# Layer 2 of a fused graph network: the reciprocal root by Sqrt and reciprocal instead of Ln, Exp and a Newton step

## The chip, the cores and the metric

The kernel runs on one core of one Trainium2 chip. The core has a matrix engine (TensorE, PE in the profile), VectorE (DVE), ScalarE (ACT), GpSimd (POOL) and a queue for transfers (SyncE, SP). The metric is the device time of one launch in microseconds (us), lower is better. The kernel before takes 2618.51 us, the median of 3 runs (2617.28 to 2624.15).

## The reference

The input is a batch of 32 graphs with 512 nodes of 64 features each, an adjacency matrix of 512 x 512 per graph (symmetric in its pattern), and a node mask. Four graph layers follow one another for each graph, with residuals and layer norms between them:

- layer 0 multiplies by the degree-normalised adjacency,
- layer 1 is a Chebyshev filter of order 4,
- layer 2 is hyperbolic attention: for every pair of nodes a logarithmic map, its attention weight, and a weighted sum,
- layer 3 takes weighted quantiles of each node's neighbours.

The change lies in layer 2 alone. What it must compute for a pair is

```
sub = mobius_add(-p1, p2, c)
sub_norm = maximum(norm(sub), 1e-15)
log = 2 / lambda(p1) * arctanh(clip(sub_norm, -1 + 1e-7, 1 - 1e-7)) * sub / sub_norm
```

So a norm, its reciprocal, and an inverse hyperbolic tangent are needed for each of the 512 x 512 pairs. The kernel gets all of them from two products per pair: with E a squared distance and X = E times a denominator, the norm is E/sqrt(X), and the inverse tangent is half the difference of two logarithms, ln(1 + s) - ln(1 - s). The function is symmetric in the two nodes, so only the upper block triangle is worked out: 1280 columns for the 128 rows of a tile, in two parts of 640.

## The kernel before

The 32 graphs are independent until the end. For each graph the program records some 1,100 operations in several lanes: `front` (layers 0 and 1), `pairs` and `tail` (layer 2), `graph` (the adjacency pattern, ranks and slots that layer 3 needs), `gather` and `sort` (bringing the neighbours' values together and sorting them in a network of minima and maxima), and, for each two graphs, `head` (quantiles and the last dense layers). Nothing is issued while recording. The class `Order` then lays out all operations of all graphs in one list per engine: `issue` (line 295) steps through a model of five clocks, gives each operation a cost that its helper states (line 445 for VectorE, 482 for ScalarE, 504 for TensorE, 468 for GpSimd), and takes, on the engine whose clock is earliest, the ready operation with the earliest due time. Due times come from `STAGES` (line 1415) and a period of 80 us for each graph. The order found is pinned, so on the chip each engine works through its list strictly in order, and waits at an instruction whose inputs are not there. Where the model sees TensorE idle, it writes filler products in (lines 1451 to 1454). The helpers' lines (448, 452, 455, 461 on VectorE, 471, 475 and 722 on GpSimd, 483 on ScalarE, 502 and 507 on TensorE) are the lines of the profile, so operations are told apart by their tiles.

The stated costs take part in the program only through the order. `recip` (line 460) costs what any f32 operation of one element per cycle costs, 0.07 us + 1.04 ns per element.

ScalarE works with one set of function tables at a time. The field `table` of an operation names the set that it needs; where the model sees a change it adds 1.28 us, and `issue` writes a load of the set with both exponential and logarithm ahead of a switch to "exp" (line 391). Loads of the set for Sigmoid and Tanh are put in by the compiler.

In `pairs` (lines 969 to 1092), per graph:

- lines 1005 to 1014: two logarithms on a 128 x 4 tile (`lp`, `sn`), then four GpSimd operations that end in `oo`, the bias of the Sigmoid on line 1077.
- lines 1038 to 1046: TensorE gives the distances; ScalarE writes E, VectorE writes X, over four blocks of rows.
- lines 1049 to 1052: in both parts of 640 columns, ScalarE writes R = exp(-0.5 ln(X + tiny)) and W = 0.5 R squared.
- lines 1053 to 1060: VectorE makes one Newton step, R = (W X - 1.5) R, whose sign comes out negative; then E = E R, and the clip as a maximum with -1 + 1e-7. ScalarE takes the two logarithms from it.
- lines 1061 to 1092: the difference of the logarithms times R gives Q; then logits, Sigmoid, adjacency, and the weighted sum.

The tiles EX, RW, FT, Q of this lane have one buffer each.

Of the kernel before, what the change touches and what calls it, by code (L numbers as in the profile page):

```python
# [8 lines left out]
F32 = mybir.dt.float32  # L9
# [5 lines left out]
AF = mybir.ActivationFunctionType  # L15
OP = mybir.AluOpType
# [4 lines left out]
P = 128  # L21
# [159 lines left out]
class Order:  # L181
# [41 lines left out]
            self.masks[key] = m  # L223
        return a.tensor.name, p, p + a.ap[0][1], m

    def op(self, engine, issue, tail, fn, outs, ins, table=None):

        if not self.on:
            fn()
            return  # L230
        i = len(self.ops)
        deps, names = {}, set()
        for a, write in [(a, False) for a in ins] + [(a, True) for a in outs]:
            if a is None or not isinstance(a, bass.AP) or a.space == DRAM:
                continue
            name, p0, p1, m = self.region(a)
            if name in self.tiles:
                names.add(name)
            elif name not in self.seen and not write:
                continue  # L240
            w, r = self.seen.setdefault(name, ([], []))
            for e in w:
                if e[2] & m and e[0] < p1 and p0 < e[1]:
                    deps[e[3]] = True
            if write:
                for e in r:
                    if e[2] & m and e[0] < p1 and p0 < e[1]:
                        deps.setdefault(e[3], False)
                for k in (w, r):
                    for e in k:  # L250
                        if p0 <= e[0] and e[1] <= p1:
                            e[2] &= ~m
                    k[:] = [e for e in k if e[2]]
                w.append([p0, p1, m, i])
            else:
                r.append([p0, p1, m, i])
        if engine == "PE":

            name, p0, p1, _ = self.region(outs[0])
            g = self.groups.setdefault(name, [])  # L260
            for e in g:
                if e[0] < p1 and p0 < e[1]:
                    deps.setdefault(e[2], False)
            g[:] = [e for e in g if not (p0 <= e[0] and e[1] <= p1)] + [(p0, p1, i)]
        deps.pop(i, None)
        for n in names:
            self.tiles[n][2] += 1
        self.ops.append((engine, issue, tail, fn, deps, names, (self.lane, self.batch), table))

    def due(self, period, stage):  # L270


        end, depth, longest = [0.0] * len(self.ops), [0.0] * len(self.ops), {}
        for i, (e, issue, tail, _, deps, _, where, _) in enumerate(self.ops):
            t = 0.0
            for d, full in deps.items():
                if self.ops[d][6] == where:
                    t = max(t, self.after(d, i, end[d], full))
            depth[i] = t
            end[i] = t + issue  # L280
            longest[where] = max(longest.get(where, 0.0), t + issue)
        key = []
        for i, o in enumerate(self.ops):
            (lane, b), (lo, hi) = o[6], stage[o[6][0]]
            key.append(period * (b + lo + (hi - lo) * depth[i] / longest[o[6]]))
        return key
# [8 lines left out]
    def issue(self, period, stage, filler, fill):  # L295
        import heapq

        ops, n = self.ops, len(self.ops)
# [16 lines left out]
        table = None  # L315
# [4 lines left out]
        while len(order) < n:  # L320
            best = None
            for e in self.ENGINES:
                t = clock[e] if ready[e] or e == "PE" and any(shapes.values()) else max(clock[e], coming[e][0][0]) if coming[e] else None
# [3 lines left out]
            t, e = best  # L327
            clock[e] = t
            while coming[e] and coming[e][0][0] <= t:
                i = heapq.heappop(coming[e])[1]  # L330
                heapq.heappush(shapes.setdefault(ops[i][7], []) if e == "PE" else ready[e], (key[i], i))
            if e == "PE":
                pick = min((h[0][0] + (0.0 if c == shape else self.STAY), c) for c, h in shapes.items() if h)[1]
                i = heapq.heappop(shapes[pick])[1]
            else:
                i = heapq.heappop(ready[e])[1]
            engine, issue, tail, fn, deps, names, where, tab = ops[i]
# [24 lines left out]
            elif tab is not None and tab != table:  # L362
                switch, table = True, tab
# [18 lines left out]
        before, spare = {}, 0.0  # L382
        for t, _, i, tab in sorted(order):
            e, fn = ops[i][0], ops[i][3]
            if e == "PE":

                for _ in range(int((t - spare - fill) / 0.11)):
                    before[e] = self.pin(filler(), before.get(e))
                spare = t + ops[i][1]
            if tab == "exp":  # L390
                before[e] = self.pin(self.nc.scalar.preload_act_table_set("natural_log_exp_and_others"), before.get(e))
            before[e] = self.pin(fn(), before.get(e))
        self.span = max(clock.values()), order

# [9 lines left out]
def tile_adj_resnorm(ctx: ExitStack, tc: tile.TileContext, x, adj, nodemask, w1k, b1k, att_w, att_b,  # L404
                     w1, b1, w2, b2, out):
    nc = tc.nc
# [12 lines left out]
    const = ctx.enter_context(tc.tile_pool(name="const", bufs=1))  # L419
# [5 lines left out]
    seq = Order(nc, tc)  # L425
# [21 lines left out]
    def tt(out, a, b, op):  # L447
        vec(lambda: nc.vector.tensor_tensor(out, a, b, op=op), out, [a, b])  # L448

    def ts(out, a, s1, s2, op0, op1=None):  # L450
        kw = {} if op1 is None else {"op1": op1}
        vec(lambda: nc.vector.tensor_scalar(out, a, s1, s2, op0=op0, **kw), out, [a], True, (s1, s2))  # L452

    def stt(out, a, s, b, op0, op1):
        vec(lambda: nc.vector.scalar_tensor_tensor(out, a, s, b, op0=op0, op1=op1), out, [a, b], False, (s,))  # L455
# [4 lines left out]
    def recip(out, a):  # L460
        vec(lambda: nc.vector.reciprocal(out, a), out, [a])
# [4 lines left out]
    def gp(f, out, ins):  # L466

        seq.op("POOL", 1.0, 0.5, f, [out], ins)

    def gtt(out, a, b, op):  # L470
        gp(lambda: nc.gpsimd.tensor_tensor(out, a, b, op=op), out, [a, b])

    def gts(out, a, s1, s2, op0, op1=None):
        kw = {} if op1 is None else {"op1": op1}
        gp(lambda: nc.gpsimd.tensor_scalar(out, a, s1, s2, op0=op0, **kw), out, [a] + [x for x in (s1, s2) if isinstance(x, bass.AP)])

    def act(out, a, f, bias=None, scale=1.0, accum_out=None, after=None):
        sc = [x for x in (bias, scale) if isinstance(x, bass.AP)]
        kw = {k: v for k, v in (("bias", bias), ("accum_out", accum_out)) if v is not None}
        n = width(out)  # L480
        table = "exp" if f in (AF.Ln, AF.Exp) else "sig" if f in (AF.Sigmoid, AF.Tanh) else None
        seq.op("ACT", 0.12 + n * 0.83e-3 + 0.09 * len(sc) + (0.2 if accum_out is not None else 0.0),
             0.3, lambda: nc.scalar.activation(out, a, f, scale=scale, **kw), [out, accum_out], [a, after] + sc, table)  # L483

    def onehot(out, a, minus, pool):

# [119 lines left out]
    ts(last, kf[:, 16:].unsqueeze(2).to_broadcast([P, K - 16, 8]), 2.0, 1.0, op0=OP.mult, op1=OP.add)  # L606
    mhalf = const.tile([P, T], F32, name="mhalf")
    nc.gpsimd.memset(mhalf, -0.5)
    tiny = const.tile([P, 1], F32, name="tiny")
    nc.vector.memset(tiny, 1e-36)  # L610
    onesb = const.tile([P, P], BF16, name="onesb")
    nc.vector.memset(onesb, 1.0)
    zero = const.tile([P, 2 * P], BF16, name="zero")
# [28 lines left out]
    attb = rows(att_b, 1, "attb", P)  # L642
# [64 lines left out]
    def col(name):  # L707
        return seq.tile(pools["small"], [P, T], F32, name, 2)
# [260 lines left out]
    def pairs(b, res):  # L969
# [21 lines left out]
        al, gam, dn = col("al"), col("gam"), col("dn")  # L991
# [6 lines left out]
        sn = col("sn")  # L998
# [3 lines left out]
        rsn = rsqrt(sn, "rsn")  # L1002
        gtt(sn, sn, rsn, op=OP.mult)
        gts(sn, sn, 1.0 - 1e-7, None, op0=OP.min)
        lp = col("lp")
        act(lp, sn, AF.Ln, bias=1.0)
        act(sn, sn, AF.Ln, bias=1.0, scale=-1.0)
        gtt(gam, gam, rsn, op=OP.mult)
        gtt(gam, gam, xwa, op=OP.mult)
        gtt(gam, gam, hh, op=OP.mult)  # L1010
        gtt(lp, lp, sn, op=OP.subtract)
        gtt(lp, lp, gam, op=OP.mult)
        oo = col("oo")
        gts(oo, lp, 0.5, attb, op0=OP.mult, op1=OP.add)


        hx = col("hx")
        gtt(hx, hh, xwb, op=OP.mult)
# [16 lines left out]
        E, X = EX[:, 0, :], EX[:, 1, :]  # L1035
        RW = seq.tile(mid, [P, 2, NS], F32, "RW", 1)
        R, W = RW[:, 0, :], RW[:, 1, :]
        for j in range(T):
            n = N - j * P
            o = slice(OB[j], OB[j + 1])  # L1040
# [5 lines left out]
            stt(X[:, o], pt[:, :n], TINY, E[:, o], op0=OP.max, op1=OP.mult)  # L1046

        parts2 = [slice(0, OB[1] + P), slice(OB[1] + P, NS)]
        for o in parts2:
            act(R[:, o], X[:, o], AF.Ln, bias=tiny)  # L1050
            act(R[:, o], R[:, o], AF.Exp, scale=-0.5)
            act(W[:, o], R[:, o], AF.Square, scale=0.5 ** 0.5)
        for o in parts2:

            tt(W[:, o], W[:, o], X[:, o], op=OP.mult)
            stt(R[:, o], W[:, o], -1.5, R[:, o], op0=OP.add, op1=OP.mult)
            tt(E[:, o], E[:, o], R[:, o], op=OP.mult)
            ts(E[:, o], E[:, o], -1.0 + 1e-7, None, op0=OP.max)
            act(W[:, o], E[:, o], AF.Ln, bias=1.0)
            act(X[:, o], E[:, o], AF.Ln, bias=1.0, scale=-1.0)  # L1060
        Q = seq.tile(mid, [P, T, N], F32, "Q", 1)
        for o in parts2:
            tt(W[:, o], W[:, o], X[:, o], op=OP.subtract)
        for j in range(T):
            o = slice(OB[j], OB[j + 1])
# [37 lines left out]
        v = wide("v")  # L1103
# [311 lines left out]
    STAGES = {"front": (-0.6, -0.5), "pairs": (1.2, 1.3), "tail": (0.2, 1.5), "graph": (0.9, 1.0), "gather": (2.7, 2.9),  # L1415
              "sort": (4.5, 4.6), "head": (4.7, 5.6), "ends": (4.0, 4.5), "check": (3.4, 4.8)}

    nc.scalar.preload_act_table_set("natural_log_exp_and_others")
    with ExitStack() as fast:
        def pool(name, bufs, **kw):  # L1420
            pools[name] = fast.enter_context(tc.tile_pool(name=name, bufs=bufs, **kw))
# [199 lines left out]
    with tc.If(flagv > 0):  # L1621
        with ExitStack() as slow:
# [24 lines left out]
            for h in range(4):  # L1647
                t = cst.tile([P, T, QC * ROWS], BF16, name=f"parts{h}")
# [5 lines left out]
            for h in range(2):  # L1654
                f = cst.tile([P, D], F32, name=f"fold{h}")
# [49 lines left out]
```

## Time and profile before

| | |
|---|---|
| runs, median (lowest to highest) | 2618.51 us (2617.28 to 2624.15) |
| profiled execution, its span | 2620.2 us |
| PE, busy | 2458.2 us, 94% |
| DVE, busy | 2402.7 us, 92% |
| ACT, busy | 1879.2 us, 72% |
| POOL, busy | 815.8 us, 31% |
| granted TensorE clock | 0.982 of full |
| from one graph to the next (two reciprocals of `pairs`, 31 steps apart: 69.8 and 2416.1 us) | 75.7 us |
| ACT table loads: at the start, at line 391, put in at line 483 | 1, 54, 54 of 1.283 us |

The page of the profile gives no other time for that execution than its span. Busy time counts overlapping instructions once: on DVE and ACT one instruction begins some 0.08 to 0.1 us before the one ahead of it has ended, so what an instruction takes from its engine is the distance from its start to the next start, and its listed duration is that much longer. A busy PE is not a PE at its peak, and some 1081 of its products are the fillers.

### The profile page before, as it was taken

Reading aid. Unit: us, or ns where it says so; the run is one execution under the profiler, and the core shown is the slowest. Engines: PE = TensorE matmul, PEld = TensorE weight load, DVE = VectorE, ACT = ScalarE, POOL = GpSimd, SP = SyncE. Lnnn points to the kernel's source line nnn. Section 1 sums busy time; section 2 is a strip of 40 time slices with the busy share of each in tenths; the row PEclk is TensorE's granted clock in tenths of the full one; section 3 lists DMA queues with packets and bytes.
Section 4 is the critical chain, followed back from the end, with each engine's and each line's share of the span. In section 5 each row is a group of like instructions: output and inputs, shape, how many; then the busy total and the mean of one; then the engine's idle time right before and its main releaser. Section 6 shows DMA issues by size and latency. Waiting matters only on the chain.

```text
span 2620.2 us, 55667 instructions
## 1 busy us (share of the span) xinstructions
PE 2458.2 (94%) x19641; PEld 1635.4 (62%) x19667; DVE 2402.7 (92%) x9002; ACT 1879.2 (72%) x4406; POOL 815.8 (31%) x1783
## 2 busy tenths in 40 slices
PE   7999999999999999999999999999999999999997
PEld 6666566666666666666656666566666666666655
DVE  3668998999999999999999999999999999998996
ACT  5666677767777777767777677777777778776761
POOL 1233332332343333322333233333323333332210
PEclk9999999999999999999999899999999999998999
DMA  1100000000000000000000000000000000000000
GB/s 38 33 23 21 17 14 15 25 22 23 18 11 22 20 25 21 24 17 13 20 21 25 19 19 13 20 23 22 26 19 13 18 19 26 19 11 3 5 7 8
DMA packets 119723, 49.96 MB, mean 19 GB/s; under 512 B 53740, under 2 KB 119436, under 8 KB 119436
## 3 DMA queue, kind: packets, MB, share of 16 engines
q1 hardware_dynamic: 118272, 46.15, 6.4%
q8 instruction: 156, 2.56, 0.4%
q14 instruction: 131, 1.07, 0.1%
q10 hardware_dynamic: 1164, 0.18, 0.0%
HBM read 37.93 MB, written 8.39 MB: 18 GB/s over the span
## 4 chain that ended last, share of the span: by engine, by line
DVE 72%; PE 18%; ACT 6%; issue 2%; POOL 2%; DMA 0%; ACTq 0%; DVEq 0%
DVE SB L448 17%; DVE SH L448 8%; DVE gather_oh L452 6%; PE front_bank L502 5%; DVE pairs_Q L448 4%; PE gather_bank L502 3%; PE graph_bank L502 3%; DVE pairs_RW L448 3%; PE pairs_bank L502 3%; DVE sort_prod L448 3%; DVE pairs_Wt L455 3%; DVE pairs_L L455 2%; DVE tail_v L448 2%; DVE pairs_EX L448 2%; DVE pairs_RW L455 2%
## 5 line engine op out<-in xcount | busy, mean ns | idle before, releaser
L448 DVE TENSOR_TENSOR SB<-SB 128x448 f32<-128x448 f32 (+11 forms) x1424 | 565.8, 424 | 12.2 <-ACT SB L483 0.7
L502 PE MATMUL gather_bank<-gather_oh,tail_x3h 128*64 128x448 f16 (+5 forms) x5376 | 516.5, 321 | 4.8 <-ACT SB L483 3.4
L502 PEld LDWEIGHTS <-tail_x3h 128*64 128x64 bf16 x5376 | 296.0, 111 | 214.3 <-issue 112.8
L448 DVE TENSOR_TENSOR SH<-SH 128x32 f32<-128x32 f32 (+11 forms) x1744 | 347.4, 246 | 8.1
L502 PE MATMUL pairs_bank<-pairs_FT 67*128 67x512 f32 (+7 forms) x768 | 316.9, 516 | 18.7 <-ACT pairs_EX L483 7.1
L452 DVE TENSOR_SCALAR gather_oh<-graph_slot 128x256 f16<-128x256 f16 (+9 forms) x864 | 252.3, 337 | 25.3 <-PE gather_bank L502 23.5
L502 PE MATMUL front_bank<-front_AT,front_y 128*64 128x512 f32 x768 | 189.5, 607 | 18.5 <-DVE front_y L448 17.0
L502 PEld LDWEIGHTS pairs_bank<-pairs_FT 67*128 67x128 f32 (+1 forms) x768 | 130.2, 194 | 83.2 <-issue 19.7
L502 PE MATMUL graph_bank<-graph_perm,graph_V 128*128 128x512 f16 x512 | 141.0, 382 | 16.1 <-DVE graph_perm L452 13.8
L502 PEld LDWEIGHTS <-graph_nbT 128*128 128x128 f16 x1536 | 113.1, 99 | 57.6 <-issue 17.3
L722 POOL TENSOR_TENSOR front_rs<-front_var,mhalf 128x4 f32<-128x4 f32 x64 | 83.4, 1303 | 201.8 <-DVE front_var L452 152.9
L502 PEld LDWEIGHTS front_bank<-XA,front_AT 128*128 128x128 f32 x1024 | 126.0, 194 | 13.6 <-issue 6.3
L1453 PE MATMUL PA<-zero 128*128 128x256 bf16 x973 | 132.9, 278 | 0.1
L502 PE MATMUL pairs_bank<-FLS,pairs_Wt 128*128 128x66 f32 x1024 | 124.7, 274 | 3.9 <-DVE pairs_Wt L455 3.8
L502 PEld LDWEIGHTS pairs_bank<-FLS,pairs_Wt 128*128 128x128 f32 x1024 | 120.6, 192 | 10.9 <-DVE pairs_Wt L455 7.8
L502 PE MATMUL front_bank<-XA,front_AT 128*128 128x65 f32 x1024 | 124.5, 274 | 0.0
L448 DVE TENSOR_TENSOR pairs_RW<-pairs_RW,pairs_EX 128x640 f32<-128x640 f32 x128 | 104.1, 815 | 18.7 <-ACT pairs_RW L483 18.4
L502 PEld LDWEIGHTS <-tabs 128*128 128x128 f16 x1296 | 78.3, 100 | 64.2 <-issue 54.9
L502 PEld LDWEIGHTS front_bank<-front_AT,front_y 128*64 128x64 f32 x768 | 54.5, 137 | 95.6 <-issue 63.0
L483 ACT ACTIVATE graph_VP<-graph_bank 128x512 f16<-128x512 f32 x128 | 75.5, 590 | 53.7 <-PE graph_bank L502 49.4
L483 ACT ACTIVATE SB<-gather_bank 128x448 f32<-128x448 f32 (+2 forms) x192 | 81.3, 438 | 43.4 <-PE gather_bank L502 43.0
L502 PE MATMUL head_bank<-head_PT,sort_ap 128*64 128x512 f32 x240 | 111.2, 608 | 0.1
(354 smaller groups left out, 6569.8 us busy)
## 6 DMA issues: line engine op xcount, KB each, us to landing
front_A<-in_adj_dram SPq DMA_DIRECT2D x128, 256.0 KB, 2.7
XA<-in_x_dram SPq DMA_DIRECT2D x32, 128.0 KB, 2.2
xs<-tail_x SPq DMA_DIRECT2D x32, 128.0 KB, 1.9
out_dram<-head_zo SPq DMA_DIRECT2D x31, 128.0 KB, 2.0
out_dram<-tail_ends SPq DMA_DIRECT2D x1, 128.0 KB, 2.1
wk<-in_L_gnn_weight_dram ACTq DMA_DIRECT2D x1, 64.0 KB, 3.0
w1s<-in_L_gnn_W_dram ACTq DMA_DIRECT2D x2, 32.0 KB, 2.0
attw<-in_L_gnn_att_W_dram ACTq DMA_DIRECT2D x2, 0.2 KB, 3.2
```

The lines of the kernel that those rows point to most:

```text
L448: vec(lambda: nc.vector.tensor_tensor(out, a, b, op=op), out, [a, b])
L452: vec(lambda: nc.vector.tensor_scalar(out, a, s1, s2, op0=op0, **kw), out, [a], True, (s1, s2))
L455: vec(lambda: nc.vector.scalar_tensor_tensor(out, a, s, b, op0=op0, op1=op1), out, [a, b], False, (s,))
L483: 0.3, lambda: nc.scalar.activation(out, a, f, scale=scale, **kw), [out, accum_out], [a, after] + sc, table)
L502: return nc.tensor.matmul(out, w, a, start=start, stop=stop)
L722: seq.op("POOL", 0.8, 0.6, lambda: nc.gpsimd.tensor_tensor(y, v, mhalf, op=OP.pow), [y], [v])
L1453: return nc.tensor.matmul(PA[:, 2 * P:], zero[:, :P], zero, start=False, stop=False)
```

## The change

The reciprocal root becomes ScalarE's Sqrt and VectorE's reciprocal; the Newton step goes, and with it the Square. The sign of E R becomes positive. The clip becomes a Relu: with under = 1 - 2^-23, t = Relu(under - E R), and then ln(1 + s) = ln(double - t) and ln(1 - s) = ln(t + least), with double = 2 - 2^-23 and least = 2^-23 as bias tiles. Both logarithms of a part, and the small `lp` and `sn`, are recorded as `behind` the two roots, so that the model never puts a logarithm between two roots. The table sets are now three: "root", "log", "sig". The load written ahead of a switch is now that of the plain logarithm set; the loads for Sqrt and for Sigmoid are put in by the compiler.

```diff
-    def op(self, engine, issue, tail, fn, outs, ins, table=None):
+    def op(self, engine, issue, tail, fn, outs, ins, table=None, behind=()):
...
-        deps, names = {}, set()
+        deps, names = {d: False for d in behind}, set()
...
+        return i
...
-            if tab == "exp":
-                before[e] = self.pin(self.nc.scalar.preload_act_table_set("natural_log_exp_and_others"), before.get(e))
+            if tab == "log":
+                before[e] = self.pin(self.nc.scalar.preload_act_table_set("natural_log"), before.get(e))
...
-        table = "exp" if f in (AF.Ln, AF.Exp) else "sig" if f in (AF.Sigmoid, AF.Tanh) else None
+        table = "log" if f == AF.Ln else "sig" if f in (AF.Sigmoid, AF.Tanh) else "root" if f == AF.Sqrt else None
...
+    tiny = constant("tiny", 1e-36)
+    least, under, double = constant("least", 2.0**-23), constant("under", 1.0 - 2.0**-23), constant("double", 2.0 - 2.0**-23)
...
-        lp = col("lp")
-        act(lp, sn, AF.Ln, bias=1.0)
-        act(sn, sn, AF.Ln, bias=1.0, scale=-1.0)
...
-        gtt(lp, lp, sn, op=OP.subtract)
-        gtt(lp, lp, gam, op=OP.mult)
-        oo = col("oo")
-        gts(oo, lp, 0.5, attb, op0=OP.mult, op1=OP.add)
...
         parts2 = [slice(0, OB[1] + P), slice(OB[1] + P, NS)]
+        roots = [act(R[:, o], X[:, o], AF.Sqrt, bias=tiny) for o in parts2]
         for o in parts2:
-            act(R[:, o], X[:, o], AF.Ln, bias=tiny)
-            act(R[:, o], R[:, o], AF.Exp, scale=-0.5)
-            act(W[:, o], R[:, o], AF.Square, scale=0.5 ** 0.5)
-        for o in parts2:
-
-            tt(W[:, o], W[:, o], X[:, o], op=OP.mult)
-            stt(R[:, o], W[:, o], -1.5, R[:, o], op0=OP.add, op1=OP.mult)
+            recip(R[:, o], R[:, o])
             tt(E[:, o], E[:, o], R[:, o], op=OP.mult)
-            ts(E[:, o], E[:, o], -1.0 + 1e-7, None, op0=OP.max)
-            act(W[:, o], E[:, o], AF.Ln, bias=1.0)
-            act(X[:, o], E[:, o], AF.Ln, bias=1.0, scale=-1.0)
+            act(E[:, o], E[:, o], AF.Relu, bias=under, scale=-1.0)
+            act(W[:, o], E[:, o], AF.Ln, bias=double, scale=-1.0, behind=roots)
+            act(X[:, o], E[:, o], AF.Ln, bias=least, behind=roots)
+        lp = col("lp")
+        act(lp, sn, AF.Ln, bias=1.0, behind=roots)
+        act(sn, sn, AF.Ln, bias=1.0, scale=-1.0, behind=roots)
+        gtt(lp, lp, sn, op=OP.subtract)
+        gtt(lp, lp, gam, op=OP.mult)
+        oo = col("oo")
+        gts(oo, lp, 0.5, attb, op0=OP.mult, op1=OP.add)
```

In the built program the counts differ as the diff says, and in nothing else but two: per graph VectorE loses two TENSOR_TENSOR, two SCALAR_TENSOR_TENSOR and two TENSOR_SCALAR of 128 x 640 and gains two RECIPROCAL of 128 x 640; ScalarE loses one ACTIVATE of 640 columns in each part. The table loads go from 109 to 97 (one at the start, then 32 for each of the three sets), and TensorE's fillers from 1081 to 1152. The order of all engines is laid out anew, since the model's costs changed.

## The prediction

> **What bounds the kernel now.** I read the page first: busy time by engine, then the chain of work that ended last.
>
> ```profile
> span 2620.2 us, 55667 instructions
> ...
> PE 2458.2 (94%) x19641; PEld 1635.4 (62%) x19667; DVE 2402.7 (92%) x9002; ACT 1879.2 (72%) x4406; POOL 815.8 (31%) x1783
> ...
> DVE 72%; PE 18%; ACT 6%; issue 2%; POOL 2%; DMA 0%; ACTq 0%; DVEq 0%
> ```
>
> Two engines are nearly full, and the chain says which of them decides: 72% of the span goes through VectorE, 18% through TensorE, only 6% through ScalarE. To take out the ramp at both ends I asked for the sums of the stretch from 200 to 2600 us (its length comes first, then PE, PEld, DVE, ACT, POOL).
>
> ```profile
> 200.00:2600.00 2400.00, 2268.09 (x18197) 1496.68 (x18221) 2290.24 (x8566) 1747.65 (x4123) 765.47 (x1596) 0.98 0.07 18
> ```
>
> VectorE is busy for 2290.24 of 2400 us, 95.4%; TensorE for 94.5%. One graph follows another every 75.7 us, so VectorE works 72.2 us per graph and idles 3.5. The waits of VectorE show why it idles: mostly for TensorE (17.1 us in all for `front_bank` under `front_st`, 23.5 us for `gather_bank`), and 18.4 us for ScalarE's Exp and Square in `pairs`. So VectorE is the bound, TensorE is right behind it, and ScalarE has 28% to spare. What the change is worth is read from VectorE.
>
> **What VectorE loses.** The groups of instructions with shapes kept apart (count, busy us, mean ns, idle before):
>
> ```profile
> L448 DVE TENSOR_TENSOR pairs_RW<-pairs_RW,pairs_EX 128x640 f32<-128x640 f32 x128 | 104.1, 815 | 18.7 <-ACT pairs_RW L483 18.4 <-ACT pairs_EX L483 0.2
> L455 DVE SCALAR_TENSOR_TENSOR pairs_RW<-pairs_RW 128x640 f32<-128x640 f32 x64 | 52.3, 817 | 0.3
> L452 DVE TENSOR_SCALAR pairs_EX<-pairs_EX 128x640 f32<-128x640 f32 x64 | 30.9, 483 | 0.0
> L448 DVE TENSOR_TENSOR SH<-SH 128x8 f32<-128x8 f32 x120 | 17.2, 158 | 0.5
> L461 DVE RECIPROCAL pairs_dn<-pairs_dn 128x4 f32<-128x4 f32 x32 | 5.3, 167 | 0.0
> L448 DVE TENSOR_TENSOR graph_c<-graph_c,graph_do 128x4 f32<-128x4 f32 x32 | 4.9, 154 | 0.2
> ```
>
> Of the first row half goes (W X; the difference of the logarithms stays), of the second and third all: 64 of each. Listed durations overlap with the next instruction. How much, the timeline shows where VectorE's instructions stand back to back:
>
> ```profile
> 1058.42 0.82 DVE L448 TENSOR_TENSOR pairs_RW<-pairs_RW,pairs_EX 128x640 f32<-128x640 f32 x1
> 1059.15 0.82 DVE L448 TENSOR_TENSOR pairs_EX<-pairs_EX,pairs_RW 128x640 f32<-128x640 f32 x1
> 1059.89 0.69 DVE L448 TENSOR_TENSOR pairs_Q<-pairs_RW 128x512 f32<-128x512 f32 x1
> ...
> 1089.84 0.17 DVE L461 RECIPROCAL pairs_hinv<-pairs_hh 128x4 f32<-128x4 f32 x1
> 1089.93 0.26 DVE L448 TENSOR_TENSOR SB<-SB 128x132 f32<-128x132 f32 x1
> ```
>
> From start to start a product of 640 takes 0.735 us, 0.08 less than listed. So each part loses 0.735 + 0.735 + (0.483 - 0.08 = 0.40) = 1.87 us of VectorE, and the 64 parts lose 120 us.
>
> **What VectorE gains: the cost that decides.** 64 reciprocals of 128 x 640. The trace has none of that size, only 128 of 128 x 4, at 166 to 169 ns. Two TENSOR_TENSOR rows give the ordinary rate: (815 - 158) / (640 - 8) = 1.04 ns per element and 150 ns fixed. A two-input operation of four elements takes 154 ns, as that line says; the reciprocal of four takes 168, 14 ns more. Two readings:
>
> - the 14 ns are paid per instruction: then 640 elements take 0.735 + 0.014 = 0.75 us from start to start, and the reciprocal costs what one product cost;
> - the 14 ns are paid per element, 3.5 ns each on top of 1.04: then 640 elements take 0.15 + 640 x 4.5 ns = 3.03 us, 2.95 from start to start.
>
> Here a rule speaks against the change. The Trainium skill, "VectorE: DVE Perf Modes", section "Walkthrough: the 8-slice pipeline in each mode", says that Reciprocal is an iterative hardware division with a repeat count of 8. Read as eight cycles for each element, where the ordinary rate of 1.04 ns is one cycle, an element would take 8.3 ns and a part 0.15 - 0.08 + 5.33 = 5.40 us. But then four elements would take 150 + 33 = 183 ns, and the row says 168. So the rule's literal price is contradicted by the row, while its point, that work is repeated per element, fits the 14 ns. It makes the second reading likelier than the first. Nothing in the row suggests a reciprocal cheaper than a product; the floor, if it ran two elements per cycle as the TENSOR_SCALAR of 640 does, would be 0.40 us.
>
> I take 2.95 us, the row drawn out in proportion; the ends are 0.40 and 5.40. Then a part changes by 2.95 - 1.87 = +1.08 us, and VectorE by 64 x 1.08 = **+69 us**. With 0.75 it would be -72 us, with 5.40 +226 us.
>
> **How much of +69 us reaches the end.** VectorE would work 72.2 + 2.16 = 74.4 us per graph, against a period of 75.7. Were its idle 3.5 us per graph all waits for others that run out when it falls behind, little would be seen; were its share of 95.4% kept, the period would be 78.0, +2.3 us, over 31 periods +71. Neither holds: TensorE gets ahead and is waited for less, but the order was laid out with a reciprocal of 0.07 + 640 x 1.04 ns, 0.74 us, so each comes 2.2 us later than planned for those behind it. In the built order the Relu, which waits for reciprocal and product, has on ScalarE's queue behind it a `graph_slot` eviction, the second root, a table load, `graph_dist` and the eviction of `gather_bank` into SB; TensorE waits for that bank. This stall is the same lateness seen from another engine, not added. I take 85%: 0.85 x 69 = **+59 us**.
>
> **ScalarE and the rest.** Each part loses Exp and Square, 0.63 us each from start to start (two of them begin at 1055.71 and 1056.34 where they stand next to another 640), and gains a Relu with bias tile, 828 ns listed as the Ln with `tiny`, 0.73; the two logarithms get a bias tile each, 828 instead of 735, +0.09. Sum -1.26 + 0.73 + 0.18 = -0.35 us, 64 parts: -22 us. Twelve loads fewer at 1.283: -15 us. The Trainium skill, "ScalarE: Activation LUTs", section "What ACT_TABLE_LOAD costs", adds 1.38 us of drain to each, so -32 us; the trace has the load at 1081.20 and the next activation at 1082.49, no such gap, so I take -15. Either way 37 to 54 us leave an engine that carries 6% of the chain: 0 on the end, hidden under VectorE, and at most those 6% of it, 3 us, if it is not. The logarithms that now stand behind both roots delay a part's W by at most the time to the second root; VectorE has merges in SB and SH to work on meanwhile, as the 18.4 us in 15 waits for the old Exp and Square show; that cost is 0 to +18 us, taken as 0, since the old wait of the same size is gone. `lp`, `sn` and four GpSimd operations move later; they are needed only by the Sigmoid, some 25 ACTIVATEs further in the built order: 0. GpSimd is busy 31%. No DMA is added or moved. 71 more fillers fall into planned idle time of TensorE: 0.
>
> Sum, against the profiled span: 2620.2 + 59 = 2679. The median of the runs is 1.7 us below that span, so **2677 us**.
>
> **The rivals.** A difference under 0.3% (8 us) is about what a measurement of this kernel can't tell from no change.
>
> - *The 14 ns are fixed* (30%). Then VectorE loses 72 us and has 69.9 us per graph. TensorE becomes the bound: at 94.5% it works 71.6 us per graph, and much of its 4 us of idle is waiting for VectorE (22.0 us for `front_st`, 17.0 for `front_y`, 13.8 for `graph_perm` in all). I give half of the 72: 2582 us. For it: a reciprocal at one element per cycle with a longer pipeline would show just this row. This one ends on the other side; it decides once a reciprocal of 640 costs less than the 1.87 us that it replaces.
> - *The literal rule* (10%). +226 us, and with VectorE then alone the bound nine tenths count: 2618.5 + 203 = 2822 us. Against it: the 168 ns.
> - *Absorbed* (6%). The reciprocal costs 2.95 us, but VectorE fills up to the 99% that it reaches in its best stretch (99.14 of 100 us from 1800 on): 74.4 / 0.99 = 75.2 us per graph, no slower than now: within 8 us of 2618.5.
>
> That the change doesn't do what it says is out: the built program has one load per set and graph, so no logarithm falls between two roots.
>
> **How the numbers follow.** The forecast has the remaining 54%. Faster: 29 of the first rival's 30. Slower: 54 + 10 less a little for a full absorption, 64. Same: 7. The range reaches down to the first rival's time and a little under, 2575, and up to what a reciprocal of 3.9 us makes, 64 x 2.03 = 130, all of it, and some more: 2760. Outside lie the literal rule and the ends of the others, not quite 2 in 10. The forecast's own range is 2635 to 2730.
>
> **What would show it.** The row RECIPROCAL pairs_RW of 128 x 640 at about 3.0 us listed, 64 times (0.83: first rival; 5.5: second). VectorE busy near 2470 us and its share of the chain over 72%; ScalarE near 1842 us busy with 97 loads; TensorE's waits for VectorE longer. The prediction is wrong if that row is short, or if VectorE's share rises to 98% and the span stays.

## The result and the profile after

The changed kernel takes 2808.62 us (median of 4 runs, 2804.97 to 2809.39) against 2621.33 us for the kernel before (2617.28 to 2635.35): a ratio of 1.0713, 95% interval 1.0688 to 1.0737. It is 187 us slower. The forecast was 2677 us, range 2575 to 2760; the time lies outside.

The page of the changed kernel's profile, first busy time and then the chain that ended last:

```profile
span 2803.1 us, 55637 instructions
...
PE 2520.4 (90%) x19712; PEld 1669.1 (60%) x19738; DVE 2551.4 (91%) x8877; ACT 1849.9 (66%) x4330; POOL 780.5 (28%) x1783
...
DVE 72%; PE 20%; ACT 5%; issue 2%; POOL 1%; DMA 0%; ACTq 0%; DVEq 0%
```

The span grew by 182.9 us. VectorE is busy 148.7 us longer (2402.7 before), and the rest of the span, in which it is not busy, grew by 34.2 us, from 217.5 to 251.7. A forecast that counts on idle time being used up should have seen that second number fall. ScalarE is 29 us less busy, and nothing came of it.

The groups with shapes kept apart give the new row and what is left of the old ones:

```profile
L462 DVE RECIPROCAL pairs_RW<-pairs_RW 128x640 f32<-128x640 f32 x64 | 265.3, 4146 | 20.1 <-ACT pairs_RW L484 20.1
L449 DVE TENSOR_TENSOR pairs_EX<-pairs_EX,pairs_RW 128x640 f32<-128x640 f32 x64 | 52.4, 818 | 0.9
L449 DVE TENSOR_TENSOR pairs_RW<-pairs_RW,pairs_EX 128x640 f32<-128x640 f32 x64 | 51.6, 813 | 3.3 <-ACT pairs_EX L484 3.2
```

And the timeline of VectorE shows one of them with its successor:

```profile
1053.61 4.14 DVE L462 RECIPROCAL pairs_RW<-pairs_RW 128x640 f32<-128x640 f32 x1
1057.67 0.36 DVE L449 TENSOR_TENSOR tail_v<-tail_v,tail_u 128x256 f32<-128x256 f32 x1
```

A reciprocal of 640 elements is listed at 4.146 us and keeps VectorE from start to start for 4.06. It replaces instructions worth 1.87 us. So VectorE's own loss is 64 x (4.06 - 1.87) = 140 us, twice the 69 that the prediction has.

Who waits has changed too. First TensorE's waits, then one of VectorE's, then ScalarE's longest, all in the changed kernel (us in all, times, longest):

```profile
PE front_bank L503 <- DVE front_y L449: 53.3, 38, 5.7
PE sort_bank L503 <- DVE sort_prod L449: 30.0, 18, 4.9
PE gather_bank L503 <- ACT SB L484: 20.9, 16, 2.8
...
DVE gather_oh L453 <- PE gather_bank L503: 46.2, 26, 3.9
...
ACT pairs_EX L484 <- DVE pairs_EX L449: 144.2, 52, 6.4
```

The first four in the kernel before:

```profile
PE front_bank L502 <- DVE front_y L448: 17.0, 28, 1.9
PE sort_bank L502 <- DVE sort_prod L448: 8.4, 13, 1.9
PE gather_bank L502 <- ACT SB L483: 3.4, 7, 0.9
...
DVE gather_oh L452 <- PE gather_bank L502: 23.5, 18, 3.0
```

The last of the changed kernel's is the new wait of the Relu. TensorE waits longer for VectorE, as foretold; but VectorE also waits longer for TensorE, which was not.

### The profile page after: what moved, and what is told of

Its sections match the earlier page's. It is cut to its first block, busy times and chain, and to the rows that moved or that the text cites. A ratio compares the mean times of both kernels' runs of the same rounds, so it can differ in the third digit from the quotient of the medians.

```text
span 2803.1 us, 55637 instructions
## 1 busy us (share of the span) xinstructions
PE 2520.4 (90%) x19712; PEld 1669.1 (60%) x19738; DVE 2551.4 (91%) x8877; ACT 1849.9 (66%) x4330; POOL 780.5 (28%) x1783
## 4 chain that ended last, share of the span: by engine, by line
DVE 72%; PE 20%; ACT 5%; issue 2%; POOL 1%; DMA 0%; ACTq 0%; DVEq 0%
DVE SB L449 16%; DVE pairs_RW L462 9%; DVE SH L449 9%; DVE gather_oh L453 6%; PE front_bank L503 6%; PE gather_bank L503 3%; PE graph_bank L503 3%; DVE pairs_Q L449 3%; PE pairs_bank L503 3%; DVE pairs_Wt L456 2%; DVE sort_prod L449 2%; DVE pairs_L L456 2%; DVE pairs_EX L449 2%; DVE tail_v L449 1%; PE head_bank L503 1%
## 5 line engine op out<-in xcount | busy, mean ns | idle before, releaser
L503 PE MATMUL gather_bank<-gather_oh,tail_x3h 128*64 128x448 f16 (+5 forms) x5376 | 526.8, 324 | 21.2 <-ACT SB L484 20.9
L449 DVE TENSOR_TENSOR SH<-SH 128x128 f32<-128x128 f32 (+11 forms) x1744 | 346.2, 246 | 9.5 <-ACT SH L484 1.3
L503 PE MATMUL pairs_bank<-pairs_FT 67*128 67x512 f32 (+7 forms) x768 | 310.1, 507 | 21.1 <-DVE pairs_EX L456 11.7
L462 DVE RECIPROCAL pairs_RW<-pairs_RW 128x640 f32<-128x640 f32 x64 | 265.3, 4146 | 20.1 <-ACT pairs_RW L484 20.1
L503 PE MATMUL front_bank<-front_AT,front_y 128*64 128x512 f32 x768 | 219.1, 692 | 55.2 <-DVE front_y L449 53.3
L484 ACT ACTIVATE pairs_EX<-pairs_EX,under 128x640 f32<-128x640 f32 x64 | 53.0, 827 | 158.6 <-DVE pairs_EX L449 144.2
L503 PEld LDWEIGHTS front_bank<-front_AT,front_y 128*64 128x64 f32 x768 | 60.9, 154 | 146.7 <-issue 87.2
```

The costliest lines, as they stand in the source:

```text
L503: return nc.tensor.matmul(out, w, a, start=start, stop=stop)
```

## The experiments

The first theory: two causes, the rate of the reciprocal and the order, laid out with 0.74 us for an instruction of 4.06. Its rivals: the rate alone; other parts of the change; ScalarE's queue held at the Relu; TensorE's clock; the luck of one order. Each run is beside runs of the kernel before on the same chip; ratios carry their 95% interval.

**The price put right (e1_priced).**

```diff
     def recip(out, a):
-        vec(lambda: nc.vector.reciprocal(out, a), out, [a])
+        seq.op("DVE", 0.045 + width(out) * 6.25e-3, 0.085, lambda: nc.vector.reciprocal(out, a), [out], [a])
```

> The changed kernel, laid out with a reciprocal priced at 0.045 us + 6.25 ns per element (4.05 us for 640), as the profile of the changed kernel shows it, instead of 0.74 us. Nothing else differs but the order. Theory 'rate and order': of the 187 us lost, about 140 are VectorE's own added time (64 x (4.06 - 1.87)), the other 45 come from an order laid out for a short reciprocal; then this takes about 2760 us (2745 to 2775). Theory 'rate alone' (the order is of no weight, VectorE's time is simply paid with the idle share it always had): about 2805 us.

Measured: 2724.98 us, ratio 1.0404 (1.0371 to 1.0437). The same instructions with a true price in the plan take 84 us less, and less than either theory gave; the rate alone does not explain the changed kernel. Its page and its waits (VectorE's for `gather_bank`; TensorE's for `front_y` and `sort_prod`):

```profile
span 2724.0 us, 56775 instructions
...
PE 2533.2 (93%) x20283; PEld 1695.2 (62%) x20283; DVE 2534.8 (93%) x8877; ACT 1854.6 (68%) x4334; POOL 782.2 (29%) x1783
...
DVE gather_oh L453 <- PE gather_bank L503: 17.2, 15, 3.0
...
PE front_bank L503 <- DVE front_y L449: 17.0, 24, 2.8
PE sort_bank L503 <- DVE sort_prod L449: 11.6, 16, 2.6
```

The three waits are back to about what they were before the change. VectorE is not busy for 189.2 us, 28 less than before and 62 less than in the changed kernel. Here the idle time is used up in part: of the 140 us added, 104 reach the span.

**A product in the reciprocal's place (e2_product).**

```diff
-            recip(R[:, o], R[:, o])
+            tt(R[:, o], R[:, o], R[:, o], op=OP.mult)
```

> The changed kernel in exactly its own order, with each of the 64 reciprocals of 128 x 640 replaced by a product of the same tile with itself (0.735 us from start to start); the reciprocal is left out, so the values are not the layer's. Theory 'the reciprocal is the whole loss': VectorE then carries 72 us less than before the change and the kernel takes 2575 to 2600 us, faster than before. Theory 'the three table sets, the bias tiles or the order itself cost as well': 2620 us or more.

Measured: 2610.45 us, ratio 0.9974 (0.9963 to 0.9984). The order is the changed kernel's instruction for instruction, so 198 us, all of its loss, come with the 64 reciprocals, for 64 x (4.06 - 0.735) = 213 us of VectorE. The kernel without them is not slower than the kernel before. But the other half of this reading is as important: VectorE carries 72 us less than in the kernel before and only some 9 come out, between what the two theories gave. What the table sets, the bias tiles and this order cost by themselves is therefore not shown to be nothing; it could be part of the missing 63. The page of this run:

```profile
PE 2472.6 (95%) x19738; PEld 1656.7 (63%) x19738; DVE 2347.4 (90%) x8877; ACT 1843.7 (70%) x4330; POOL 807.8 (31%) x1783
...
DVE 60%; PE 28%; ACT 8%; issue 2%; POOL 1%; DMA 0%; ACTq 0%; DVEq 0%
```

VectorE's share of the chain falls from 72 to 60% and TensorE's rises from 18 to 28%: TensorE took over a part of the chain.

**Half of them (e9_half).**

```diff
-            recip(R[:, o], R[:, o])
+            if o.start == 0:
+                recip(R[:, o], R[:, o])
+            else:
+                tt(R[:, o], R[:, o], R[:, o], op=OP.mult)
```

> The changed kernel in exactly its own order, with the second part's reciprocal replaced by a product (0.735 us) and the first part's kept: 32 reciprocals instead of 64; the second part's values are not the layer's. With none it took 2610 us, with 64 it took 2808. Theory 'each reciprocal costs the same': 2709 us. Theory 'the first microseconds on VectorE are absorbed, because TensorE is the bound there': 2660 to 2690 us. Theory 'any unplanned stall costs at once': 2720 us or more.

Measured: 2724.51 us, ratio 1.0404 (1.0385 to 1.0423). The first 32 reciprocals cost 114 us, the other 32 cost 84, each time for 106 us of VectorE. Nothing is absorbed: in an order that does not know of them, these 32 cost a little more than themselves. They are those of each graph's first part; the second part's alone were not run.

**The Relu freed of the reciprocal (e3_relu_free).**

```diff
...
-            tt(E[:, o], E[:, o], R[:, o], op=OP.mult)
-            act(E[:, o], E[:, o], AF.Relu, bias=under, scale=-1.0)
-            act(W[:, o], E[:, o], AF.Ln, bias=double, scale=-1.0, behind=roots)
-            act(X[:, o], E[:, o], AF.Ln, bias=least, behind=roots)
+            done = tt(E[:, o], E[:, o], R[:, o], op=OP.mult)
+            act(W[:, o], X[:, o], AF.Relu, bias=under, scale=-1.0, behind=[done])
+            act(X[:, o], W[:, o], AF.Ln, bias=least, behind=roots)
+            act(W[:, o], W[:, o], AF.Ln, bias=double, scale=-1.0, behind=roots)
```

> The changed kernel with all reciprocals, in its own order but for the two logarithms of a part changing places, with the Relu reading X and writing W, so that ScalarE no longer waits for the reciprocal; the logarithms are then not those of the norm (the product of distance and reciprocal is made but not used by them). Theory 'ScalarE's queue is held at the Relu and passes the lateness on to TensorE's banks and back to VectorE': VectorE's idle time falls back towards 212 us and the kernel takes about 2770 us. Theory 'the lateness of VectorE itself is all there is': no change, 2800 to 2810 us.

Measured: 2808.34 us, ratio 1.0722 (1.0688 to 1.0756): no change. ScalarE's 144 us at the Relu are gone; its longest waits are now for TensorE, and TensorE's for VectorE is longer still:

```profile
ACT front_sums L484 <- PE front_bank L503: 123.5, 53, 8.4
...
PE front_bank L503 <- DVE front_y L449: 78.3, 39, 7.1
```

The new wait was large, and taking it away gains nothing. That the lateness reaches TensorE straight from VectorE is the reading that the waits suggest.

**Is it TensorE's clock? (e13_warm, and e6_priced_nofill)** In the changed kernel the granted clock, as a share of full speed, is 0.956, against 0.982 before. The products of `front_y` show it; before and after, by tile (ns: shortest, median, longest):

```profile
L502 PE MATMUL front_bank<-front_AT,front_y x768: 591/592/1116, 42.7 to 2385.9; 128*64 128x512 f32 x192
```

```profile
L503 PE MATMUL front_bank<-front_AT,front_y x768: 592/592/1117, 42.2 to 2568.9; 128*64 128x512 f32 x192
```

The two rows look alike: there are two speeds, 592 ns and about half of that rate. What differs is how many are slow: counted over 700 ns, 8 of 768 before, 161 in the changed kernel, 36 with the true price, 4 with the product. They follow gaps: sorted by the longest idle time of TensorE in the 8 us ahead of them, of the changed kernel's 768 products none of 382 is slow behind gaps under 1 us, 32 of 150 behind 1 to 2 us, 51 of 132 behind 2 to 3, and 78 of 104 behind over 3. The Trainium skill, "TensorE: Matmul & The Clock Gate", section "Part 1: The HAM clock gate (the "warmup" mystery)", has the clock fall to half after an idle window of about 3.4 us; the trace agrees on the half, and shows slow products behind shorter gaps too. So I put fillers into the 102 gaps of over 0.7 us that the changed kernel's profile shows, at their places in TensorE's order, and nowhere else:

```diff
...
+                for _ in range(WARM.get(nth, 0)):
+                    before[e] = self.pin(filler(), before.get(e))
+                nth += 1
                 spare = t + ops[i][1]
```

> The changed kernel in its own order, with fillers put on TensorE at the 102 places (from 200 us on) where its profile shows TensorE idle for over 0.7 us: 1342 fillers, as many as fit into each gap less 0.3 us. Theory 'the unplanned stalls cool TensorE's clock, and its slow products pass the lateness on': products after front_y at over 700 ns fall from 161 to under 50, TensorE's other work from 2512 us to about 2470, and the kernel takes 2760 to 2785 us. Theory 'the stall itself, not the clock, is the loss': slow products fall, but the kernel takes 2800 us or more.

Measured: 2792.61 us, ratio 1.0655 (1.0609 to 1.0702); slow products 161 to 23. The answers on the cores, of the changed kernel and of this one:

```profile
core 0: 2803.1 us, clock 0.956
```

```profile
core 0: 2792.2 us, clock 0.984
```

The clock is wholly restored, and TensorE's busy time, counted without the fillers' lines, falls from 2394 to 2343 us. Only 16 of the 84 us come back, between what the two theories gave. The clock is a part, a small one, as far as this run can show: the fillers have a fixed number, so where a gap would have become shorter they hold it open.

The other way about, fillers taken out of the order with the true price:

```diff
-                for _ in range(int((t - spare - fill) / 0.11)):
+                for _ in range(0 if 200.0 < t < 2400.0 else int((t - spare - fill) / 0.11)):
...
```

> The laid out with the true price of the reciprocal (2725 us), and TensorE's fillers left out between 200 and 2400 us of the plan: 828 of 1697 remain, the order of everything else is the same. Theory 'the fillers keep TensorE's clock up': products after front_y at over 700 ns, 36 of 768 with fillers, rise well over 100, and the kernel takes 2760 us or more. Theory 'the gain over the changed kernel is the order, and fillers are dead weight': 2700 to 2725 us, and few slow products.

Measured: 2739.48 us, ratio 1.0452 (1.0392 to 1.0511), 67 slow products: 14 us lost with 869 fillers, neither theory's number. The granted clock falls from 0.977 to 0.956, that of the changed kernel, and the loss agrees in size with the 16 of the run before.

**The Relu alone, on the kernel before (e4_relu_alone, e7_relu_nofill).**

```diff
...
-            ts(E[:, o], E[:, o], -1.0 + 1e-7, None, op0=OP.max)
-            act(W[:, o], E[:, o], AF.Ln, bias=1.0)
-            act(X[:, o], E[:, o], AF.Ln, bias=1.0, scale=-1.0)
+            act(E[:, o], E[:, o], AF.Relu, bias=under)
+            act(W[:, o], E[:, o], AF.Ln, bias=least)
+            act(X[:, o], E[:, o], AF.Ln, bias=double, scale=-1.0)
```

> The kernel before with one part of the change alone: the clip as a Relu on ScalarE with bias tiles for the two logarithms, Newton step and exponential kept. VectorE loses 64 x 0.40 = 26 us, ScalarE gains 64 x 0.91 = 58 us. Theory 'VectorE is the bound and ScalarE has room': 2595 to 2605 us. Theory 'TensorE takes over at once, or ScalarE's waits do': 2615 to 2630 us.

Measured: 2656.62 us, ratio 1.0153 (1.0115 to 1.019). Both theories missed: VectorE has 26 us less to do, and the kernel is 37 us slower. Its order has 281 fillers more than the one before, so I took the middle ones out, with the edit of e6_priced_nofill:

> The Relu alone on the kernel before (2657 us, 1362 fillers), with the fillers between 200 and 2400 us of the plan left out: 750 remain, the order of everything else is the same. Theory 'the 281 fillers more than before take TensorE's own time': 2620 us or less. Theory 'the order and the 58 us more on ScalarE do it': 2645 to 2660 us. Theory 'fillers keep the clock up': slower than 2657 us.

Measured: 2662.21 us, ratio 1.0154 (1.0096 to 1.0211). Not the fillers. The order and ScalarE remain; ScalarE is in fact busy 75 us longer (1953.9), since this order also has twelve more table loads (60 and 60 in place of 54 and 54, of 1.28 us each).

**What an order alone can do (e10_before_hop, e11_after_hop, e12_priced_hop).** One constant of the plan, the time that it allows from an engine to the next, no work changed:

```diff
-    HOP = 0.1
+    HOP = 0.11
```

> The kernel before, its plan's allowance between engines at 0.11 instead of 0.10 us: no work is changed, the order of all engines is laid out anew. It gives the size of what a new order alone can do. Theory 'orders differ by little': 2610 to 2630 us. Theory 'the order before is a lucky one': 2640 us or more, as the Relu alone (2657 us) would then be explained without its cost.

> The changed kernel, the allowance at 0.11 us, the reciprocal still priced at 0.74 us. Theory 'the loss is the reciprocal and its price in the plan': 2790 to 2825 us. Theory 'the changed kernel's order is an unlucky one': 2760 us or less.

> The changed kernel laid out with the true price of the reciprocal, the allowance at 0.11 us. Theory 'the true price saves some 80 us whatever the order': 2715 to 2740 us. Theory 'the 83 us were the luck of one order': 2760 us or more.

| | allowance 0.10 | allowance 0.11 |
|---|---|---|
| kernel before | 2620.06 | 2647.21 (ratio 1.0112, 1.0094 to 1.0131) |
| changed kernel | 2808.62 | 2823.95 (ratio 1.0781, 1.0763 to 1.0799) |
| changed, true price | 2724.98 | 2732.70 (ratio 1.0441, 1.0423 to 1.0459) |
| before, no Newton step (below) | 2588.13 | 2580.72 (ratio 0.9844, 0.98 to 0.9887) |

Ratios are against the kernel before as it is, allowance 0.10. Its order is a good one: another costs it 27 us. So the 37 us of the Relu alone are mostly of a size that an order makes, and stay unexplained beyond that. The loss of the changed kernel is not: in the second column it is 177 us, of which the true price saves 91.

**The rate by itself (e5_sizes).**

```diff
+    for n in (1, 2, 4, 8, 16, 64, 160, 320, 640):
+        for _ in range(4):
+            nc.vector.reciprocal(rou[:, :n], rin[:, :n])
+    for n in (4, 640):
+        for _ in range(4):
+            nc.vector.tensor_tensor(rou[:, :n], rin[:, :n], rin[:, :n], op=OP.mult)
     setup.close()
```

> The kernel before with reciprocals of 1, 2, 4, 8, 16, 64, 160, 320 and 640 f32 elements per partition (four each, back to back) and four products of 4 and of 640 in the setup. If the price per element is the same at all sizes, start to start grows by 6.25 ns per element from the smallest on, 4 elements take about 88 ns and the line through 4 and 640 (0.088 and 4.063 us) holds for all: 0.16 at 16, 0.46 at 64, 1.06 at 160, 2.06 at 320 us. If short ones run at another rate (4.5 ns per element, as the prediction drew it), there is a bend between 4 and 640.

One execution took 2629.06 us, the setup's reciprocals included. The groups:

```profile
L1416 DVE RECIPROCAL rou<-rin 128x640 f32<-128x640 f32 x4 | 16.6, 4146 | 0.0
L1416 DVE RECIPROCAL rou<-rin 128x320 f32<-128x320 f32 x4 | 8.6, 2143 | 0.0
L1416 DVE RECIPROCAL rou<-rin 128x64 f32<-128x64 f32 x4 | 2.2, 548 | 0.1
L1416 DVE RECIPROCAL rou<-rin 128x16 f32<-128x16 f32 x4 | 1.0, 253 | 0.1
L1416 DVE RECIPROCAL rou<-rin 128x8 f32<-128x8 f32 x4 | 0.8, 203 | 0.1
L1416 DVE RECIPROCAL rou<-rin 128x4 f32<-128x4 f32 x4 | 0.7, 178 | 0.1
L1419 DVE TENSOR_TENSOR rou<-rin 128x4 f32<-128x4 f32 x4 | 0.6, 160 | 0.0
```

From 8 to 16 elements (203 to 253) as from 320 to 640 (2143 to 4146) an element costs 6.25 ns: a line, 153 + 6.25 n ns listed, with no bend. (At 1 and at 2 elements three of the four list 162 to 166; the fourth, 485 and 1124 ns, overlaps other work of the setup, and why it is long stays open.) But four elements by themselves take 178 ns, where the kernel before lists 166 to 169, and the product of four takes 160, where it lists 154. The kernel before shows it too: three of its 128 reciprocals began after the instruction ahead had ended and list 177 to 178 ns, the other 125 at most 173. So a row of four moves by some 10 ns with what stands ahead of it, and that is as much as the prediction read from it: 14 ns drew out to 4.5 ns an element, the 18 ns of this run (178 - 160) would draw out to 5.5.

**A version that is faster than both (e8_no_newton, e14_no_newton_hop).** If the wish is a shorter VectorE, the Newton step can go without a reciprocal coming:

```diff
             act(R[:, o], R[:, o], AF.Exp, scale=-0.5)
-            act(W[:, o], R[:, o], AF.Square, scale=0.5 ** 0.5)
...
-            tt(W[:, o], W[:, o], X[:, o], op=OP.mult)
-            stt(R[:, o], W[:, o], -1.5, R[:, o], op0=OP.add, op1=OP.mult)
             tt(E[:, o], E[:, o], R[:, o], op=OP.mult)
-            ts(E[:, o], E[:, o], -1.0 + 1e-7, None, op0=OP.max)
+            ts(E[:, o], E[:, o], 1.0 - 1e-7, None, op0=OP.min)
```

> The kernel before without the Square and the Newton step, the reciprocal root being exp(-0.5 ln) alone, the clip still on VectorE: VectorE loses 64 x 1.47 = 94 us, ScalarE 64 x 0.63 = 40 us; the step that sharpens the root is left out. Theory 'TensorE is the next bound right away' (as the product in place of the reciprocal showed: 72 us less on VectorE, 9 us less in all): 2600 to 2615 us. Theory 'VectorE's savings come through': 2540 to 2580 us.

> The kernel without Square and Newton step, laid out with an allowance of 0.11 us between engines: another order of the same work. The kernel before takes 2647 us with it. Theory 'the step's 94 us on VectorE are worth about 30 us in any order': 2600 to 2625 us. Theory 'the 31 us gained were the luck of one order': 2640 us or more.

Measured: 2588.13 us, ratio 0.9863 (0.9806 to 0.992), and in the other order 2580.72 us. Both theories of the first run bracket it: of 94 us taken from VectorE about 30 come out in the first order. In the second it is 66 against the kernel before in that order (2647.21), more than the run's two theories gave. VectorE's share of the chain is then 63%, TensorE's 25%:

```profile
PE 2436.7 (94%) x19658; PEld 1634.6 (63%) x19658; DVE 2324.4 (90%) x8874; ACT 1817.4 (70%) x4322; POOL 772.3 (30%) x1783
...
DVE 63%; PE 25%; ACT 7%; issue 2%; POOL 2%; DMA 0%; ACTq 0%; DVEq 0%
```

The gain holds in both orders, so it isn't the luck of one; its size depends on the order.

## Why the prediction was wrong

- **VectorE as the bound and what it loses, 1.87 us a part: right.** The reciprocals alone make 198 us in an unchanged order.
- **The step that failed first: "I take 2.95 us, the row drawn out in proportion".** The term is 4.06. The direction was right, that the 14 ns are paid per element, and the size was not: an element costs 6.25 ns, not 4.5. The 150 ns taken from the kernel's own rows as fixed cost are right to 3 ns (153). What was missed is 1.75 ns an element: 7 ns in a row of four, 1.1 us in one of 640. The row held that uncertainty in plain sight: its listed durations run from 139 to 178. The instruction could be costed from both sides, not to a point.
- **The literal rule, 5.40 us,** was too dear in its turn: 6.25 ns are six of the 1.04 ns that an ordinary element takes, not eight. The rival that rested on it gave 2822 us, near the measured 2809, by a wrong sum: too high a rate, and nine tenths of it.
- **The step that failed second: "I take 85%".** With the rate right that share would make 0.85 x 140 = 119 us and a forecast of 2737; the order with the true price measures 2725. For an order that knows the price the step is of the right kind and too high (106 of 140, 75%; in the second order 86, 61%). The changed kernel's order doesn't know it: there 187 us come of 140. The prediction saw the late reciprocals and named the price of 0.74, then took them for one and the same lateness. As far as ScalarE's queue goes that reading held (e3_relu_free: no change); but a wrong price in the plan costs by itself, against the true one 84 us with the one allowance and 91 with the other. Of these the cooled clock is about 16. The rest is the order: the waits for `front_y`, `sort_prod` and `gather_bank` grow on both sides, and the true price takes them back. That TensorE's and VectorE's lists expect each other at times that do not come is the reading of these waits; which of them carries how much was not taken apart.
- **The first rival** would, in the changed kernel's order, not have come true at a cheap reciprocal either: it gave half of 72 us to the end, the product in its place showed some 9. Two orders of the same work lie up to 27 us apart here, so this is one order's number.
- **ScalarE and the rest at 0:** not contradicted, and not shown. With all of the change but the reciprocal the kernel is 9 us faster, loads and bias tiles included, but VectorE has 72 us less to do there. The old wait for Exp and Square (18.4 us) is not gone, as the prediction had it: VectorE waits 20.1 us for the roots, and 3.2 for the logarithms (0.2 before). In sum that is 5 us more.
- The range's upper end came from 3.9 us for a reciprocal with all of it on the path; it left out that a wrong price in the plan is a loss of its own.

## What to carry to other kernels

A price read from a four-element row does not carry to 640 elements: before an operation is put on wide tiles, run it once at the real width. Where a planner lays out the order, a new instruction is a new entry in its price list; with the wrong price this kernel took 84 us longer than with the true one. And before a gain is read from the busiest engine, ask how close the next one is: 72 us less on VectorE were 9 us less in all in one run, 94 were 30 and 66 in two others.

## What the runs showed of the hardware

- VectorE's reciprocal of f32 takes 6.25 ns per element at every width from 4 to 640 (153 + 6.25 n ns listed, 4.06 us from start to start at 640), six times a product's 1.04 ns. The same root by Ln, Exp and a Newton step took VectorE 1.87 us a part, clip included.
- TensorE's products fell to half speed behind gaps of 1 to 2 us in 32 of 150 cases already, and in none of 382 behind shorter ones (in the run with half of the reciprocals in 10 of 524). The trace's record of the granted clock has it at half speed in 49 stretches, 250 us in all (14 stretches and 97 us before), each a whole multiple of 3.41 us. Of the 46 that begin after 200 us only two follow 3.41 us without a product; ahead of the others TensorE was idle for 0.7 to 3.1 us of the last 3.41. Filling 102 gaps brought the granted clock from 0.956 to 0.984 and the kernel 16 us.
- A table load on ScalarE takes 1.28 us with no gap behind it, also between Sqrt and Ln. The timeline of the changed kernel:

```profile
1052.15 0.83 ACT L484 ACTIVATE pairs_RW<-pairs_EX,tiny 128x640 f32<-128x640 f32 x1
1052.99 1.28 ACT L392 ACT_TABLE_LOAD   x1
1054.29 0.83 ACT L484 ACTIVATE pairs_RW<-pairs_EX,double 128x640 f32<-128x640 f32 x1
```
